# Layer 2 of a four-layer stack: the first expert tile's two weight gathers move from ahead of the scatters to behind them

## The chip, the cores and the metric

The kernel runs on one core of a Trainium2 chip. The metric is the device time of one execution, in microseconds (us), given as the median of the runs shown. All arithmetic is in fp32.

## The reference

The program is a stack of four layers over two images of 256 channels and 32 x 32 pixels, so 2 x 1024 tokens of 256 values. Layers 0 and 1 are attention over convolution features. Layer 2 is attention in windows of 64 tokens, then a mixture of eight experts. Layer 3 is additive attention, then another mixture. The change lies at the start of layer 2's mixture, which computes:

```python
logits = xt @ Wr + br
probs = jax.nn.softmax(logits, axis=-1)
top_p, top_idx = jax.lax.top_k(probs, 2)
weights = top_p / top_p.sum(axis=-1, keepdims=True)
...
xe = xn[None, :, :] * ln_g[:, None, :] + ln_b[:, None, :]
h = gelu(einsum('end,edh->enh', xe, W1) + b1[:, None, :])
y = einsum('enh,ehd->end', h, W2) + b2[:, None, :]
out = (weights[:, :, None] * y[of the two chosen experts]).sum(axis=1)
```

## The kernel before

**Routing by slots.** Each token goes to two of eight experts. `route` (L1240) computes, on the chip, a slot number for each of a token's two choices (`rt_slot0`, `rt_slot1`), so that the slots of one expert are contiguous and padded to tiles of 128, and for every slot tile the rows of the weight table that its expert owns (`rt_rows`). A group is one image: 1024 tokens, 8 token tiles, 23 slot tiles. `dispatch` (L1179) gates, routes and then writes the tokens out: for each token tile and each of the two choices one indirect DMA, issued on GpSimd (POOL), scatters 128 rows of 1 KB into `slots_in` in HBM (L1211). That is 16 scatters for a group. They are declared independent of each other.

**Experts.** `experts` (L1384) loops over the 23 slot tiles m. SyncE (SP) loads a tile of `slots_in` into `xr` (L1419), which needs the scatters of the group; TensorE transposes it (L1427), VectorE scales it into `xe` (L1431). `up` runs two halves of 16 matmuls against the up weights (L1452), VectorE adds the bias into `hb` (L1463), ScalarE applies GELU (L1441), `down` runs 16 matmuls against the down weights (L1472), and the result goes to `slots_out`.

**Weights.** A tile's expert is known only at run time, so its weights are gathered by an indirect DMA on POOL, in `fetch` (L1365, the DMA is recorded at L1370): `l2_up` with 128 rows of 2056 values, `l2_down` with 128 rows of 2048, so about 1.05 MB each. There are three pairs of buffers (`ew00`, `ew01`, `ew10` and so on); tile m uses pair m modulo 3. Where the rows say that the buffer already holds the same expert, the row numbers are out of bounds and nothing is moved. At its first step `experts` asks for the inputs of tiles 0, 1 and 2, and for up 0, down 0, up 1, down 1, up 2; what is already in `self.fetched[key]` is left out. In the loop, tile m asks for down m+2 and up m+3.

**What orders the work.** Up to the first expert tiles of layer 2, the order on POOL, SP and VectorE isn't the program's: the tile framework places instructions by their program priority and by when they become ready. In the window attention (`window_attention`, which runs `dispatch(2, 0)` as the generator `route`, a few steps in each of its last rounds) the order on TensorE and ScalarE is the program's. The rest of the stack is merged from generators by a plan with due times (`run`, L1752): `E20` is `experts(2, 0)`, due at 0; `D21` is `dispatch(2, 1)`, the other image's group, due at 5. From `E21` on, TensorE, ScalarE and VectorE keep the merged order.

**What else is on POOL there.** `divide(i)` of the window attention (L895) normalises the attention weights of token tile i in two POOL instructions (`probs`, L901), one for each half of the partitions. Those of the last tile, i = 15, come earlier in the program than the gathers and scatters. TensorE's transposes of that tile (L920), its value and output matmuls (L929, L943), VectorE's addition into `t` (L946) and then the gate of group (2, 1) (L1143, L1172) hang on them.

Of the kernel before, what the change touches and what calls it, by code (L numbers as in the profile page):

```python
# [1009 lines left out]
class Late:  # L1010
# [168 lines left out]
    def dispatch(self, *key, done=0):  # L1179

        l, b = key
        tokens = GROUPS[key]
        n = len(tokens)
        nc = self.nc
        again = self.early.tile([P, n], F32, name="again", bufs=1) if l == 2 else None
        for half in range(done, n // 4):
            yield from self.gate(l, b, half)
            if l == 2:

                mv, rs = self.last_norm  # L1190
                to = again[:, 4 * half : 4 * half + 4]
                nc.vector.tensor_tensor(to, mv[:, :, 1], rs, ALU.mult)
                nc.vector.tensor_tensor(to, to, rs, ALU.mult)
        u = self.u[key]
        if l == 2:

            rs = self.inverse_root(again, 1e-5)
            yield 3.0
            for i in range(n):
                nc.scalar.activation(u[:, i, :], u[:, i, :], AF.Identity, scale=rs[:, i : i + 1])  # L1200
            yield 5.0
        yield from self.route(key, n)
        p, shares, slots, rows = self.routes[key]
        if key == (2, 0):
            self.fetch(key, 0)
            self.fetch(key, 0, 1)

        before = []
        for i in range(n):
            for slot in slots:  # L1210
                ins = nc.gpsimd.indirect_dma_start(  # L1211
                    out=self.stack.slots_in[b % 2],
                    out_offset=bass.IndirectOffsetOnAxis(ap=slot[:, i : i + 1], axis=0),
                    in_=u[:, i, :], in_offset=None,
                ).ins
                for other in before:
                    self.tc.declare_no_dep(ins, other, reason="a slot takes one token")
                before.append(ins)
            yield None if l == 2 else 0.5
# [664 lines left out]
```

## Time and profile before

| what | us |
|---|---|
| median of three runs | 2880.11 |
| their range | 2879.3 to 2883.23 |
| the profiled execution, its own time | 2838.24 |
| its span, first to last instruction | 2836.5 |
| TensorE busy in the span | 2619.5 |
| VectorE, ScalarE, POOL busy | 1925.6, 1830.9, 1237.0 |

The profile is of one execution. Its times count from the span's first instruction, so the stretch of interest, the seam between the window attention and the experts of layer 2, lies at 1758 to 1810 us. A row of the timeline gives start, length, engine, line, operation and tiles, then in brackets how long the engine had been idle and what ended that. "POOL DMA_INDIRECT" is the instruction that issues an indirect DMA, not its transfer. "Chain" is the chain of waits that ended last, followed back from the end. PEld is TensorE's weight load, SPq an issue on SyncE's queue.

### The profile page before, as it was taken

The page shows a single profiled execution, that of the slowest core. Times are in us where ns is not written, and L with a number is a line of the kernel's source. Part 1 is how long each engine was busy: PE and PEld are TensorE (multiplying, and loading weights), DVE is VectorE, ACT ScalarE, POOL GpSimd, SP SyncE. Part 2 cuts the span into 40 slices and gives each one's busy share as a digit, 9 for nine tenths or more (in the row PEclk, how much of TensorE's full clock was granted, in tenths as well). Part 3 has the DMA queues.
Part 4 walks back from the last instruction along what each step waited for, and adds up shares of the span by engine and source line. Part 5 has one row for each costly group of instructions (what it writes and reads, how often), then busy time and mean ns, then how long its engine had stood idle before and what let it go on. Part 6 is the DMA issues. An engine that isn't in the chain of part 4 may idle for free. (4 is left out here: it accounts for less than half of the span.)

```text
span 2836.5 us, 77376 instructions
## 1 busy us (share of the span) xinstructions
PE 2619.5 (92%) x32010; PEld 1643.1 (58%) x32010; DVE 1925.6 (68%) x3579; ACT 1830.9 (65%) x2723; POOL 1237.0 (44%) x1303
## 2 busy tenths in 40 slices
PE   7899999999999999699999786899999999999997
PEld 3455555555555555455555454899666633455686
DVE  5999999999999999378778667443522343124242
ACT  2777877787787878255555343211599899989732
POOL 4877777777787777001111242343311021202152
PEclk9999999999999999899999897899999999999998
DMA  3000000000000000101110000443222010422354
GB/s 136 3 3 3 3 3 3 3 3 3 3 3 3 3 3 3 49 21 25 25 25 17 19 9 24 170 149 98 84 81 80 23 34 14 152 68 88 102 188 123
DMA packets 180705, 131.26 MB, mean 46 GB/s; under 512 B 131248, under 2 KB 162496, under 8 KB 173184
## 3 DMA queue, kind: packets, MB, share of 16 engines
q0 software_dynamic: 29232, 81.71, 8.7%
q1 hardware_dynamic: 148096, 44.25, 7.0%
q8 instruction: 251, 4.11, 0.6%
q14 instruction: 102, 0.84, 0.1%
q10 hardware_dynamic: 3024, 0.35, 0.1%
HBM read 181.11 MB, written 29.49 MB: 74 GB/s over the span
## 5 line engine op out<-in xcount | busy, mean ns | idle before, releaser
L188 ACT ACTIVATE sc<-sc,sa_shift 128x1024 f32<-128x1024 f32 x512 | 584.4, 1144 | 155.9 <-DMA sa_shift<-sa_min 153.8
L201 DVE STREAM_TRANSPOSE wt<-sc 128x1024 f32<-128x1024 f32 x512 | 601.8, 1208 | 0.2 <-ACT sc L188 0.2
L1670 ACT ACTIVATE th<-front,qb 128x1024 f32<-128x1024 f32 x512 | 539.9, 1134 | 51.4 <-PE ps_e L1679 45.3
L211 PEld LDWEIGHTS ps_o<-wt,v 128*64 128x64 f32 x8192 | 444.2, 137 | 188.0 <-issue 106.2
L143 PE MATMUL ps_s<-kT,qT 64*32 64x512 f32 x8192 | 528.0, 595 | 17.4 <-ACT sc L153 16.8
L211 PE MATMUL ps_o<-wt,v 128*64 128x128 f32 x8192 | 504.8, 276 | 26.0 <-DVE oT L372 25.4
L166 POOL TENSOR_TENSOR fold<-sc 128x512 f32<-128x512 f32 x256 | 328.8, 1285 | 196.5 <-ACT sc L153 182.7
L168 POOL TENSOR_TENSOR fold<-sc,fold 128x512 f32<-128x512 f32 x256 | 328.3, 1282 | 21.4
L153 ACT COPY sc<-ps_s 128x1024 f32<-128x1024 f32 x256 | 255.9, 1000 | 108.3 <-PE ps_s L143 55.5
L1452 PEld LDWEIGHTS ps_h<-xe,ew 128*128 128x128 f32 x2320 | 277.4, 194 | 56.6 <-issue 32.5
L150 DVE TENSOR_SCALAR_CACHE_REDUCE sc<-ps_s 128x1024 f32<-128x1024 f32 x256 | 304.6, 1190 | 7.2 <-PE ps_s L143 6.6
L1679 PE MATMUL ps_e<-th,pick 128*32 128x512 f32 x2048 | 297.6, 607 | 5.8 <-DVE sc_a L1686 4.4
L1452 PE MATMUL ps_h<-xe,ew 128*128 128x128 f32 x2320 | 293.2, 280 | 8.5 <-DVE xe L1435 7.9
L1472 PE MATMUL ps_y<-ew,h 128*128 128x256 f32 x1160 | 271.2, 383 | 3.5 <-DVE y L1476 2.2
L143 PEld LDWEIGHTS ps_s<-kT,qT 64*32 64x32 f32 x8192 | 136.2, 106 | 228.2 <-issue 161.9
L1472 PEld LDWEIGHTS ps_y<-ew,h 128*128 128x128 f32 x1160 | 212.7, 190 | 61.5 <-issue 19.6
L630 ACT ACTIVATE sc<-sc,l_least 128x1024 f32<-128x1024 f32 x128 | 146.7, 1147 | 125.8 <-DVE sc L617 125.5
L1463 DVE TENSOR_TENSOR hb<-ps_h,ew 128x512 f32<-128x512 f32 x115 | 79.4, 690 | 199.1 <-PE ps_h L1452 183.3
L1476 DVE COPY y<-ps_y 128x256 f32<-128x256 f32 x99 | 41.9, 423 | 228.1 <-PE ps_y L1472 224.0
L1441 ACT ACTIVATE h<-hb 128x512 f32<-128x512 f32 x115 | 71.5, 623 | 183.5 <-DVE hb L1463 183.4
L636 DVE STREAM_TRANSPOSE wt<-sc 128x1024 f32<-128x1024 f32 x128 | 153.3, 1224 | 46.0 <-ACT sc L630 25.4
L617 DVE TENSOR_SCALAR_CACHE_REDUCE sc<-ps_s 128x1024 f32<-128x1024 f32 x128 | 150.6, 1212 | 40.2 <-PE ps_s L609 40.0
(292 smaller groups left out, 3131.6 us busy)
## 6 DMA issues: line engine op xcount, KB each, us to landing
xr<-slots_in SPq DMA_DIRECT2D x99, 128.0 KB, 2.5
slots_out<-y SPq DMA_DIRECT2D x99, 128.0 KB, 1.7
sa_got<-sa_least SPq DMA_DIRECT2D x512, 0.5 KB, 1.8
sa_shift<-sa_min SPq DMA_DIRECT2D x512, 0.2 KB, 1.7
slots_in<-zero POOLq DMA_DIRECT2D x46, 128.0 KB, 2.6
kh<-kh SPq DMA_DIRECT2D x32, 128.0 KB, 2.3
qh<-qh SPq DMA_DIRECT2D x32, 128.0 KB, 2.3
sa_sums<-sa_total SPq DMA_DIRECT2D x244, 1.0 KB, 1.8
```

The source lines that it names most:

```text
L143: nc.tensor.matmul(ps[r][S * c : S * (c + 1), a, :].rearrange("p (b i) -> p b i", i=S), lhsT=qT[half, p, S * i : S * (i + 1)], rhs=keys[ha ...
L150: nc.vector.tensor_scalar(scores[m][0], flat[0], 1.0, None, ALU.mult, ALU.min, accum_out=least[m // 2][:, 0, h : h + 1])
L153: nc.scalar.copy(scores[m][1], flat[1])
L166: nc.gpsimd.tensor_tensor(y, a, b, ALU.subtract)
L168: nc.gpsimd.tensor_tensor(y, a, y, ALU.subtract)
L188: nc.scalar.activation(scores[m][r], scores[m][r], AF.Exp, bias=shift[m // 2][:, r : r + 1], scale=-1.0, accum_out=total[i][:, 2 * p + r, ...
L201: nc.vector.transpose(weights[i, h][:, 2 * p + r, :], x)
L211: nc.tensor.matmul(sums[i][64 * k : 64 * (k + 1)], lhsT=v[:, at % NT, 64 * (at // NT) : 64 * (at // NT + 1)], rhs=weights[i, h][:, :, S * ...
L1452: nc.tensor.matmul(ps[:, j, :], lhsT=a[:, c, at : at + P], rhs=x[:, c, :], start=(c == 0), stop=(c == CC - 1),)
L1472: nc.tensor.matmul(ps, lhsT=h[:, j, :], rhs=w2[:, j, :], start=(j == 0), stop=(j == HB - 1))
L1670: nc.scalar.activation(h, keys, AF.Tanh, bias=self.qb[b][:, s // G, g : g + 1])
L1679: nc.tensor.matmul(pe[i][c * U : (c + 1) * U, a, :], lhsT=self.pick[:, k, :], rhs=h[:, a, :], start=(k == 0), stop=(k == G - 1),)
```

## The change

After `route` has set the rows, the kernel before asks at once for both gathers of expert tile 0, ahead of the group's scatters. The changed kernel doesn't. Nothing else is edited: `experts` finds the two not fetched and issues them at its own first step, in the loop that already asks for tiles 1 and 2, after all 16 scatters.

```diff
         yield from self.route(key, n)
         p, shares, slots, rows = self.routes[key]
-        if key == (2, 0):
-            self.fetch(key, 0)
-            self.fetch(key, 0, 1)
 
         before = []
         for i in range(n):
```

The loop that now issues them, unchanged:

```python
        if l == 2:
            for m in range(lanes):
                fetch(m)
                if m < 2:
                    fetch(m, 1)
```

## Prediction

> **What bounds the kernel now.** I read four views in this order. First the chain of waits, to see which stage ends last around the change. The chain by line gives TensorE's expert matmuls (L1452, L1472) the largest shares, and the windows table shows why: once layer 2's experts run, TensorE has no idle time (columns: stretch, its length, then busy us and count of PE, PEld, DVE, ACT, POOL).
>
> ```profile
> 1795.00:1830.00 35.00, 34.39 (x233) 32.79 (x233) 15.94 (x50) 11.03 (x20) 7.97 (x8) 0.93 0.32 116
> 1830.00:1865.00 35.00, 35.00 (x248) 33.14 (x247) 14.67 (x45) 5.90 (x10) 8.97 (x9) 1.00 0.64 219
> 1865.00:1900.00 35.00, 35.00 (x247) 32.98 (x246) 17.57 (x62) 6.07 (x10) 21.13 (x21) 1.00 0.33 100
> ```
>
> So a microsecond by which the first expert tile starts earlier or later moves all 23 tiles with it, and what follows. Second, the pieces of the chain in order of time between 1740 and 1800 us, for what that start hangs on:
>
> ```profile
> 1766.46 3.45 issue
> ...
> 1786.79 2.41 DMA slots_in<-u,rt_slot
> ...
> 1789.48 4.75 DMA xr<-slots_in
> ...
> 1794.37 0.68 PE ps_x L1427 x2
> ...
> 1795.64 4.21 PE ps_h L1452 x18
> ```
>
> It hangs on the sixteenth scatter (issued 1786.79, landed 1789.2), then the load of `xr` (issued 1789.48), its transpose, the first up matmul at 1795.64. Not on weights. Third, POOL's timeline, for what delays the sixteenth scatter:
>
> ```profile
> 1763.03 0.97 POOL L1211 DMA_INDIRECT slots_in<-u,rt_slot  x1 [0.30 <-DVE rt_one L1355]
> 1764.30 1.06 POOL L1370 DMA_INDIRECT ew<-in_l_up,rt_rows  x1 [0.30 <-issue]
> 1765.43 1.03 POOL L901 TENSOR_TENSOR probs<-l,wa_rec 64x512 f32<-64x512 f32 x1
> 1770.05 1.04 POOL L901 TENSOR_TENSOR probs<-l,wa_rec 64x512 f32<-64x512 f32 x1 [3.59 <-issue]
> 1771.37 1.03 POOL L1370 DMA_INDIRECT ew<-in_l_down,rt_rows  x1 [0.28 <-POOL probs L901]
> 1772.70 1.02 POOL L1211 DMA_INDIRECT slots_in<-u,rt_slot  x1 [0.30 <-issue]
> ...
> 1786.79 0.97 POOL L1211 DMA_INDIRECT slots_in<-u,rt_slot  x1 [0.30 <-issue]
> 1788.06 1.05 POOL L1370 DMA_INDIRECT ew<-in_l_up,rt_rows  x1 [0.30 <-issue]
> ```
>
> The reader is to see both gathers of tile 0 standing in front of 12 scatters, and POOL idle for 3.59 us between the two halves of `probs`. The view says "issue", but the trace's semaphore records for POOL's sequencer hold a wait of L901 that ends at 1769.87, and the up gather's semaphore is complete at 1769.84: the second half of `probs` waits for every indirect DMA issued before it on POOL, and the gather is the last of them. Fourth, TensorE just before the start:
>
> ```profile
> 1788.82 3.75 PE L1172 MATMUL ps_router<-sb_wr,uT 128*128 128x8 f32 x16 [0.57 <-DVE uT L1144]
> 1794.37 0.66 PE L1427 MATMUL ps_x<-ident,xr 128*128 128x128 f32 x2 [1.80 <-DMA xr<-slots_in]
> ```
>
> TensorE works on the other group's gate until 1792.57 and then waits 1.80 us for `xr`. That gate is a second limit on the start.
>
> **What the Trainium skill says.** "DMA: Bandwidth & Descriptors", section "Anatomy of one DMA", prices such a DMA at 2.0 us plus its bytes over 436 GB/s: for 1.05 MB an estimate of 4.4 us. The trace has 5.5 us from the start of the 1.06 us issue instruction, so it agrees. The same page, "Queues, rings and completion order", says that an engine drains a whole packet of one queue before it turns to another. The trace fits that: `xr`, issued 1.42 us after a gather, landed at 1794.23, 0.35 us behind the gather's 1793.88, 4.75 us where the median `xr` takes 2.5. "TensorE: Matmul & The Clock Gate", section "What's actually happening", has a clock that starts at half rate and is released by a busy window of about 3.4 us in a free-running grid. The trace agrees: the clock is 0.50 from 1782.9 to 1799.95, so the first 4.3 us of expert matmuls take 421 ns each, not 275.
>
> **The change, part by part.** (a) Removed ahead of the scatters: the up gather's place on POOL, 1764.30 to the next instruction's normal start, 1.27 us (the pitch of scatters, 0.97 + 0.30); the down gather's, 1772.70 - 1771.37 = 1.33 us. (b) Removed wait: with the gather gone, a scatter takes its place at 1764.30, the first half of `probs` stays at 1765.43, and the second half waits for that scatter: 1764.30 + 2.4 (median landing) = 1766.7, plus 0.2 from semaphore to start as before, 1766.9 for 1770.05. That is 3.15 us. If `probs` comes straight after the fourth scatter the sum is the same within 0.1. (c) Sixteenth scatter: `probs` ends 1767.95, the sixth scatter starts at 1768.25, ten more pitches of 1.275 bring the sixteenth to 1781.0, for 1786.79: **5.8 us earlier**. It lands at 1783.4 and `xr` is issued at 1783.7 (call this X; before, X was 1789.48). SP's other waits there are on work of 1778.6 and before, which moves with `probs`.
>
> (d) Moved behind: six gathers now follow the scatters where four did, at 1.3 us of POOL each (1788.06, 1789.42, 1790.74 before). POOL has nothing else queued until the next gather, at 1802.74 before, so their issue is covered. Tile 0's up gather is issued at 1782.3, X - 1.4, just where tile 1's was. That row landed at X + 4.4, so tile 0's weights should land at X + 4.4, and `xr` behind them at X + 4.75. The first up matmul comes at X + 6.16, so the cover is 1.8 us. Below: nothing can be gained from a weight that wasn't waited for. Above: if the gather took the 8.5 us of the second in a row, the matmul would wait 1 us. I take zero.
>
> (e) Tile 1's up weights become third in the row. Before, the four landed at X + 4.4, 8.4, 11.0 and 13.8. Tile 1's first up matmul came after 14 of the 30 in the row at 1800.01, at 1801.65, X + 12.2. Third in the row is X + 11.0: 1.2 us of cover, and a wait of up to 1 us if the clock is full sooner. Down 0 (X + 8.4, needed X + 15.9), up 2 (about X + 16.5, needed X + 19.3) and the later ones have more.
>
> (f) What is late next: the gate. It hangs on the second half of `probs` (TensorE's L920 starts at 1771.15, 0.06 us after it), so it moves by 3.15 us, not 5.8: it ends at 1789.4, while `xr` could be transposed at 1794.37 - 5.8 = 1788.6. The start then moves by 1.80 + 3.15 = 4.95 us. If the transpose goes first, it moves by 5.8, but the 3.75 us of gate matmuls at half clock fall behind it. So 5.0 to 5.8; I take **5.3 us**. The clock is worth up to 1.7 us either way (half of one 3.4 us window), zero in the mean. From there TensorE is busy without gaps, so the end moves by the same.
>
> The profiled execution would go from 2838.24 to 2832.9. The median shown is 41.9 us above that execution; nothing in the change scales with that, so I subtract the same: 2880.1 - 5.3 = **2874.8 us**.
>
> **The rivals.** One: more gain. With the gap ahead of the start closed, the gate's matmuls and the experts' run without pause, the clock is full one window sooner, and the transpose goes first: 5.8 + 1.7 = 7.5, 2872.6 us. For it: TensorE's 1.80 us gap disappears. Against: the grid of the clock's windows isn't the program's. Two: the gathers become the wait. If the six share the DMA engines worse than the four did (at 1793 to 1796 us these were already 1.01 busy), tiles 0 and 1 wait for weights by 1 to 2 us each and about 2 us of gain stay: 2878. Three: the change doesn't do what it says, because POOL's order is by readiness (before, four scatters went ahead of a gather that stands first in the program): 2880. Four, slower: the framework, which chooses VectorE's order in advance, holds tile 0 to be late for its weights and puts the other group's routing in front of its `xe`. For it: that routing is interleaved there already. Its price: the first group's took 15.0 us from the exponential at 1743.76 to the last slot number at 1758.73. Begun at the gate's new end, 1789.4, plus 0.5 for maximum and subtraction, it puts `xe` at 1804.9 for 1795.17: 9.7 us slower, 2889.8. It decides once more than 5.7 us of routing stand in front. Against: before, most of that routing ran inside the experts (its counts matmul is at 1859).
>
> **How the numbers follow.** The forecast has 0.56, more gain 0.17, gathers as the wait 0.13, no effect 0.03, slower 0.11. A difference of 0.2%, 5.8 us, is about what a measurement of this kernel can tell from no change. The forecast's own range is 2872.5 to 2877 (the clock, and POOL's and SP's order downstream, which is placed anew), so about a third of it, 0.20, lies below 2874.3: faster 0.37, within 0.52, slower 0.11. The range goes from 2871 (rival one with a favourable order downstream) to 2880.5 (rivals two and three); outside it are rival four and about 0.07 of tails.
>
> **What would show it.** Right: on POOL 16 scatters and then six gathers in a row; 1.3 us or less of idle time between the halves of `probs`; sixteenth scatter near 1781.0, first up matmul near 1790, ended by `xe` and not by a gather; no idle TensorE after it. Wrong: a first up matmul that waits for a DMA of `ew`, gathers between the scatters, or routing instructions (L1260 to L1314) ahead of the first `xe` on VectorE.

## The result, and the profile after

The changed kernel takes 2876.42 us (median of 19 runs, 2870.28 to 2880.03) where the kernel before took 2879.44 us beside it. The ratio is 0.9984 with a 95% interval of 0.9977 to 0.9990: **4.6 us faster, 2.9 to 6.6**. (Gains below are worked out from the ratio of the runs; it isn't the quotient of the two medians, which lie 3.0 us apart.) The forecast was 5.3 us, and the time it named, 2874.8 us, is 1.6 us off.

The profiled execution of after took 2871.1 us, that of before 2838.24. Only about 6 of those 33 us are there by the middle of the first group's experts, 13 over most of the second group's and 27 over the first of layer 3's. They are not the change's: the kernel before, profiled again below, took 2831.3 us on one chip and 2879.6 on another, and those two profiles part in jumps as well. At this seam they part by 10.1 us; from tile 0 to tile 20 of the group nothing is added. So the seam is read here from the first scatter of group (2, 0): its start is subtracted from every time, and written as S + n.

The windows table of after (columns as in the prediction) shows TensorE without idle time in the experts again:

```profile
1795.00:1830.00 35.00, 34.79 (x233) 33.18 (x232) 16.97 (x56) 9.12 (x16) 6.97 (x7) 0.89 0.28 102
1830.00:1865.00 35.00, 35.00 (x242) 32.98 (x241) 15.69 (x43) 9.53 (x15) 8.96 (x9) 1.00 0.61 215
```

POOL's timeline of after:

```profile
1768.76 0.97 POOL L1208 DMA_INDIRECT slots_in<-u,rt_slot  x1 [0.30 <-DMA slots_in<-u,rt_slot]
1769.79 1.03 POOL L901 TENSOR_TENSOR probs<-l,wa_rec 64x512 f32<-64x512 f32 x1
1771.41 1.04 POOL L901 TENSOR_TENSOR probs<-l,wa_rec 64x512 f32<-64x512 f32 x1 [0.59 <-DMA slots_in<-u,rt_slot]
...
1780.41 0.97 POOL L1208 DMA_INDIRECT slots_in<-u,rt_slot  x1 [0.30 <-issue]
1781.68 1.06 POOL L1367 DMA_INDIRECT ew<-in_l_up,rt_rows  x1 [0.31 <-issue]
...
1788.27 1.00 POOL L1367 DMA_INDIRECT ew<-in_l_down,rt_rows  x1 [0.30 <-issue]
```

The sixteenth scatter starts at 1780.41, S + 22.3 (S is 1758.13), where it was S + 28.0, and six gathers follow in a row. The 3.6 us wait between the halves of `probs` has shrunk to 0.59. But nine scatters now stand ahead of `probs`, not four, so its second half comes at S + 13.3 instead of S + 11.3: later, not earlier.

The chain of waits of after, in order of time (start, length, what):

```profile
1778.35 4.77 issue
1783.12 3.06 PE ps_wo L943 x4
...
1786.33 8.14 DMA xr<-slots_in
1794.47 0.14 issue
1794.61 0.66 PE ps_x L1424 x2
1795.27 2.79 PE ps_router L1172 x14
1798.05 4.05 PE ps_h L1449 x18
```

It no longer runs through the sixteenth scatter. Further back it runs through the ninth, for which the second half of `probs` waited (1771.41). Then it runs through the last window tile's output projection (L943), the load of `xr`, its transpose, and then through **14 router matmuls of the other group's gate**, which now stand between the transpose and the first up matmul. TensorE's order has changed. Before, both halves of that gate (each 8 transposes, L1143, and 16 router matmuls, L1172) stood ahead of the first tile's transpose. Now the second half lies between the expert tiles; its last piece on TensorE's timeline of after:

```profile
1834.46 1.85 PE L1172 MATMUL ps_router<-sb_wr,uT 128*128 128x8 f32 x16
```

### The profile page after: what moved, and what is told of

Read it like the earlier page. It is cut to its first block, busy times and chain, and to the rows that moved or that the text cites. A ratio compares the mean times of both kernels' runs of the same rounds, so it can differ in the third digit from the quotient of the medians.

```text
span 2869.4 us, 77379 instructions
## 1 busy us (share of the span) xinstructions
PE 2628.3 (92%) x32010; PEld 1645.6 (57%) x32010; DVE 1925.7 (67%) x3579; ACT 1835.4 (64%) x2725; POOL 1237.8 (43%) x1303
## 5 line engine op out<-in xcount | busy, mean ns | idle before, releaser
L1449 PEld LDWEIGHTS ps_h<-xe,ew 128*128 128x128 f32 x2320 | 278.6, 195 | 63.2 <-issue 36.5
L1473 DVE COPY y<-ps_y 128x256 f32<-128x256 f32 x99 | 41.9, 424 | 230.3 <-PE ps_y L1469 213.4
L617 DVE TENSOR_SCALAR_CACHE_REDUCE sc<-ps_s 128x1024 f32<-128x1024 f32 x128 | 150.6, 1212 | 40.0 <-PE ps_s L609 39.8
```

The source lines that it names most:

```text
L1449: nc.tensor.matmul(ps[:, j, :], lhsT=a[:, c, at : at + P], rhs=x[:, c, :], start=(c == 0), stop=(c == CC - 1),)
```

## Experiments

Theory one, of the **scatters**: the sixteenth scatter sets the start of the experts, as the prediction had it. Theory two, of **probs**: with nine scatters ahead of it, the last window tile's chain has become the limit. Theory three, of the **placement**: the seam gained nothing, and the gain comes from the order of later work. Two more, of the **cover** and of the **order**, came out of the first runs.

The copy `y` that ends a tile (L1473, before L1476) is a marker for what the seam is worth: from tile 5 to the end of the group it keeps a constant distance to the kernel before. All runs stand in one table, with times as S + n. "Up" is the first up matmul's start, "gained" how much earlier `y` of tile 5 comes than in the kernel before on a chip of the same kind, and "ratio" the time over that of the kernel before, run beside it.

| kernel | 16th scatter | transpose | up | y of tile 5 | gained | ratio (95%) |
|---|---|---|---|---|---|---|
| **chip with runs near 2835** | | | | | | |
| before | 28.2 | 35.7 | 36.9 | 86.5 | | 0.9999 (0.9989 to 1.0008) |
| changed | 22.3 | 29.6 | 32.9 | 86.0 | 0.5 | 0.9997 (0.9988 to 1.0005) |
| changed, early probs | 22.2 | 29.7 | 31.0 | 83.2 | 3.3 | 0.9983 (0.9972 to 0.9994) |
| before, early probs | 24.9 | 32.5 | 33.7 | 83.2 | 3.3 | 0.9988 (0.9980 to 0.9995) |
| **chips with runs near 2880** | | | | | | |
| before | 28.0 | 45.6 | 46.9 | 96.6 | | |
| changed (the result) | 22.3 | 36.5 | 39.8 | 92.8 | 3.8 | 0.9984 (0.9977 to 0.9990) |
| up gather alone | 26.7 | 35.4 | 40.4 | 92.1 | 4.5 | 0.9980 (0.9970 to 0.9989) |
| down gather alone | 26.7 | 36.1 | 40.4 | 92.3 | 4.3 | 0.9977 (0.9966 to 0.9988) |
| changed, early probs, gate first | 22.2 | 45.6 | 46.8 | 96.6 | 0.0 | 1.0008 (1.0000 to 1.0016) |
| changed, gate first | 22.3 | 47.0 | 48.3 | 97.5 | -1.0 | 0.9999 (0.9992 to 1.0006) |
| before, TensorE's order | 28.0 | 35.4 | 43.4 | 95.7 | 0.9 | 0.9994 (0.9985 to 1.0002) |
| before, order of both engines | 28.0 | 35.7 | 37.3 | 89.4 | 7.2 | 0.9969 (0.9961 to 0.9977) |
| changed, early probs | 22.1 | 37.4 | 41.7 | 93.4 | 3.1 | 0.9983 (0.9973 to 0.9992) |

### Both kernels again, and probs early

No edit for the first two.

> The kernel before once more, unchanged, for a profile that can be laid beside that of the changed kernel (the profiled execution of before shown first was 33 us shorter than that of the changed kernel, far more than the 4.6 us between their runs). All theories expect the ratio to lie at 1.000 with an interval of about 0.2%, which says what a ratio of this many rounds can tell. In its profile: sixteenth scatter of the first group about 28 us after the first (28.0 in the first profile), second half of the last window tile's probs waiting some 3.6 us for the up gather, the first up matmul of the first expert tile about 37 us after the first scatter (36.9 in the first profile). If the later dispatches are long again only where the whole execution is, the 33 us are the execution's and not the change's.

> The changed kernel once more, for a second profile and more rounds. Theory of the scatters (the sixteenth scatter sets the start of the first expert tile): ratio 0.998, first up matmul 5 us nearer to the first scatter than in the kernel before. Theory of the probs (the scatters come 6 us earlier, but nine of them now stand ahead of the second half of probs, so that the turn of the first tile waits for the gate and for the window projection's psum): ratio 0.998 to 0.999, and in the profile the xr load is released by TensorE's window projection and not by the sixteenth scatter; the scatters are done 2 us or more before that. Theory of the placement (the order of the work later on moved, and the seam itself gained nothing): first up matmul at the same distance from the first scatter as before, the gain further on.

For the other two, `divide` keeps its second half's instruction, and the scatters from the fourth on and the gathers are held behind it; the last one does the same to the kernel before:

```diff
+                    late.halves = nc.gpsimd.tensor_tensor(
...
+                behind = key == (2, 0) and len(before) >= 3
+                with self.tc.issue_after(self.halves) if behind else nullcontext():
                     ins = nc.gpsimd.indirect_dma_start(
...
+        with self.tc.issue_after(self.halves) if key == (2, 0) else nullcontext():
             self.nc.gpsimd.indirect_dma_start(
```

> The changed kernel with GpSimd's order held: three scatters, then both halves of the last window tile's probs, then the other thirteen scatters and the six gathers. Nothing is left out. Theory of the probs: probs' second half ends about 7 us earlier than in the changed kernel (estimate 1764.6 against 1772.45 where the first scatter is at 1758.1), the window projection and the gate with it, the sixteenth scatter stays near 1780.2, the xr load is issued behind the scatters at about 1783 instead of 1786.3, the first up matmul comes 3 to 5 us earlier: ratio to the kernel before 0.9965 to 0.9975, 3 to 5 us faster than the changed kernel. Theory of the scatters: the sixteenth scatter is where it was, so the time is that of the changed kernel, 0.998. Theory of the placement: the ratio is anything between 0.997 and 1.001 and does not follow the seam.

> The kernel before, both gathers of the first tile still ahead of the scatters that follow, but the two gathers and the scatters from the fourth on held behind the second half of the last window tile's probs. Nothing is left out. It takes the wait for the up gather away and leaves the gathers' places on GpSimd: sixteenth scatter estimated at 1782.8 on the clock of the first profile of before, where it was 1786.8. Theory of the scatters: 4.0 us faster than before, ratio 0.9986. Theory of the probs: the same or slightly more, as the gate comes early too, 0.998 to 0.9986, about 1.5 to 2.6 us slower than the changed kernel with the same hold. Theory of the placement: no relation to the seam, 0.997 to 1.001.

Measured: on this chip the median of before was 2835.5 us. The two profiles of before near 2835 us agree to 0.2 us in the table's columns. The changed kernel's gain was 0.9 us, and the interval, from 3.4 faster to 1.4 slower, includes none. The theories of the scatters and of probs had expected 0.998 and 0.998 to 0.999. TensorE's timeline of the changed kernel here:

```profile
1789.02 0.66 PE L1424 MATMUL ps_x<-ident,xr 128*128 128x128 f32 x2 [5.83 <-DMA xr<-slots_in]
1789.47 2.99 PE L1172 MATMUL ps_router<-sb_wr,uT 128*128 128x8 f32 x14
1792.32 4.19 PE L1449 MATMUL ps_h<-xe,ew 128*128 128x128 f32 x18
...
1828.88 1.85 PE L1172 MATMUL ps_router<-sb_wr,uT 128*128 128x8 f32 x16
```

The transpose waits for `xr`, and `xr` was issued 2.7 us behind the sixteenth scatter, as the theory of the scatters has it; the transpose is 6.0 us earlier. Then 14 router matmuls stand ahead of the up matmul, which starts 3.3 us after the transpose where it was 1.3: 2.0 us lost. The gate's second half takes 3.24 more between the tiles (transposes 0.41, 0.38 and 0.60, routers 1.85). 6.0 - 2.0 - 3.2 leaves 0.8, and `y` of tile 5 shows 0.5. With early probs the first half is done long before, only the second half is paid, and 3.3 us stay; in the kernel before with early probs both halves fit ahead of the transpose, and it keeps all 3.3 us of its earlier scatter. So the theory of the scatters holds here for the transpose, not for the end. The two holds have about the ratios that this theory named (0.998 and 0.9986), but it had named 0.998 for the changed kernel too, whose sixteenth scatter is as early as with early probs and whose interval includes no gain. The theory of probs had wanted 0.9965 to 0.9975 with early probs. None of the three had the reason: **work that had run in TensorE's idle time now has to be paid.** This is the theory of the cover.

### The gate first, one gather alone, and before once more

The first kernel adds to the early probs that both halves of the gate come ahead of the first tile's transpose. `D21` becomes due 32 earlier and its routing waits 32 longer, so that the gate alone moves in the program; `self.gated` is the gate's last router matmul:

```diff
-            "D21": (self.dispatch(2, 1), (), 5, 3.45),
+            "D21": (self.dispatch(2, 1), (), -27, 3.45),
...
+        if key == (2, 1):
+            yield 32.0
         yield from self.route(key, n)
...
+            with self.tc.issue_after(self.gated) if key == (2, 0) and m == 0 else nullcontext():
                 for c in range(CC):
                     nc.tensor.transpose(ps[:, c, :], r[:, c * P : (c + 1) * P], self.ident)
```

> The changed kernel with GpSimd's order held as in the run with probs behind three scatters, and in addition the whole gate of the other group (both halves: 16 transposes and 32 router matmuls of the 48 on TensorE there) held ahead of the transpose of the first expert tile. Nothing is left out. Theory of the cover (the gate's second half ran in TensorE's idle time at the seam before; in the changed kernel and in the run with the earlier probs it falls behind the first tile's transpose, where TensorE has no idle time, and costs its own 2.4 to 3.0 us there): the transpose stays at 29.7 us after the first scatter, the gate's second half runs from about 22 to 28.5 us after it, the copy y of tiles 4 to 22 comes 5.4 to 6.0 us earlier than in the kernel before, relative to the first scatter, where the run with the earlier probs had 3.3: ratio 0.9978 to 0.9982. Theory of the scatters alone: as the run with the earlier probs, 3.3 us, 0.9983 to 0.9988. Theory of the placement: the lead at tile 4 is lost again later and the ratio is 0.999 or more.

The next two are the kernel before without one of its two early gathers:

```diff
         if key == (2, 0):
-            self.fetch(key, 0)
             self.fetch(key, 0, 1)
```

> One part alone: only the up gather of the first tile is moved behind the scatters; the down gather stays. Nothing is left out. Theory of the wait (any gather of weights ahead of the second half of probs on GpSimd costs the same wait): the down gather takes the up gather's place ahead of probs, the second half waits about 3.6 us as before, and the sixteenth scatter comes only one place earlier, 1.3 us (26.9 us after the first scatter for 28.2); ratio 0.9993 to 0.9998. If the wait goes with the up gather alone: sixteenth scatter 4.5 us earlier, ratio 0.998 to 0.999. Theory of the placement: no relation to the seam.

> The other part alone: only the down gather of the first tile is moved behind the scatters; the up gather stays where it was. Nothing is left out. All theories of the seam: the wait of probs' second half stays at 3.6 us, the sixteenth scatter comes one place, 1.3 us, earlier; the transpose of the first tile is limited by the gate, which ended 1.3 us ahead of it, so at most 1.3 us: ratio 0.9993 to 1.0. Together with the run above: the two parts alone sum to 2.6 us at the sixteenth scatter where both together gave 5.8; the 3.2 us left are the wait, which goes only when both go.

> The kernel before for a profile on this chip, beside the three above. All theories: sixteenth scatter 28.2 us and first up matmul 36.9 us after the first scatter, as in the two earlier profiles of before, if the chip's transfers are as fast as there; if its executions are slower (2880 instead of 2835), all distances at the seam that end in a transfer are longer, and those of the changed kernel's first profile can then be read against these.

These went to a chip where the kernel before takes 2879.4 us, as in the runs of the result, and every ratio expected for the gate and the single gathers missed. The wait did what was expected of it: with the up gather gone the down gather stood in its place, and the second half of `probs` waited 3.52 us. The sixteenth scatter came only 1.3 us earlier. Yet the kernels without the early up gather and without the early down gather gained 5.8 us (3.2 to 8.6) and 6.6 us (3.5 to 9.8), no less than both together. With the gate first, the sixteenth scatter came 5.8 us earlier and there was no gain. On these chips the time doesn't follow the scatters at all.

The profile of before there says why. TensorE's timeline, first on the chip near 2835, then on the one near 2880:

```profile
1783.76 1.94 PE L1143 MATMUL ps_tr<-ident,u 128*128 128x128 f32 x8 [3.33 <-DVE u L1132]
1786.27 3.75 PE L1172 MATMUL ps_router<-sb_wr,uT 128*128 128x8 f32 x16 [0.57 <-DVE uT L1144]
1791.32 0.66 PE L1427 MATMUL ps_x<-ident,xr 128*128 128x128 f32 x2 [1.30 <-DMA xr<-slots_in]
```

```profile
1797.24 1.94 PE L1143 MATMUL ps_tr<-ident,u 128*128 128x128 f32 x8 [8.14 <-DVE u L1132]
1799.75 3.75 PE L1172 MATMUL ps_router<-sb_wr,uT 128*128 128x8 f32 x16 [0.57 <-DVE uT L1144]
1803.35 0.67 PE L1427 MATMUL ps_x<-ident,xr 128*128 128x128 f32 x2
```

On the first, the gate's second half ends 1.3 us before `xr` comes. On the second it starts 11.4 us later after the first scatter (S is 1755.67 and 1757.77), and the transpose follows it without a wait: the first tile stands behind the gate. What delays the gate shows on VectorE, in the addition that takes the first half's router matmuls:

```profile
1780.47 0.19 DVE L1176 TENSOR_TENSOR rt_lg<-ps_router,sb_br 128x32 f32<-128x32 f32 x1 [1.72 <-PE ps_router L1172]
```

```profile
1794.40 0.19 DVE L1176 TENSOR_TENSOR rt_lg<-ps_router,sb_br 128x32 f32<-128x32 f32 x1 [8.15 <-remote]
```

By the trace those matmuls ended at 1780.43 and at 1789.10, so they were taken over after 0.04 us on one chip and after 5.3 us on the other. VectorE itself wasn't late: in the semaphore records of the second trace TensorE's count arrives at 1794.38, and the addition starts 0.02 us later. In all, the addition is 11.8 us later after the first scatter than on the first chip; some 6.5 us had been lost before it, on TensorE's and VectorE's work from the output projection on. The chain that prepares the second half (inverse root, scaling of `u`) stands behind this instruction on VectorE. The theory of the **order** follows: near 2880 us, time is set by whether the first tile stands behind the second half of that gate. Moving a gather, either one, made the framework place it otherwise.

### The order alone

Two kernels test that, one from each side. In the first no gather is moved; the gate's second half is held behind the first tile's transpose:

```diff
+                last = nc.tensor.transpose(ps[:, c, :], r[:, c * P : (c + 1) * P], self.ident)
+            if key == (2, 0) and m == 0:
+                self.first_turn = last.ins
...
+            with self.tc.issue_after(self.first_turn) if key == (2, 1) and 4 in tiles else nullcontext():
                 for k, i in enumerate(tiles):
                     nc.tensor.transpose(ps[:, k, :], self.u[key][:, i, c * P : (c + 1) * P], self.ident)
```

> The kernel before with its gathers where they were, and one thing changed: on TensorE the second half of the other group's gate (8 transposes, 16 router matmuls counted as the profile counts passes) is held behind the transpose of the first expert tile, where the changed kernel has it, instead of ahead. Nothing is left out. Theory of the order (what moved the time on the chip with runs near 2880 us is that the first tile no longer stands behind that half of the gate on TensorE; on the chip with runs near 2835 us the gate fitted into idle time and is only paid for elsewhere): near 2880 us, the first up matmul comes 6 to 8.5 us earlier relative to the first scatter, of which about 3 are paid back by the gate between the tiles, ratio 0.998 to 0.999, with no gather moved; near 2835 us, the first up matmul is where it was and the tiles from 5 on come 2.5 to 3 us later, ratio 1.0008 to 1.0012. Theory of the scatters: the sixteenth scatter is where it was, so no gain on either chip, 1.000 to 1.001.

The second is the changed kernel with the hold of "gate first" and nothing else.

> The changed kernel with one thing undone: on TensorE the whole gate of the other group is held ahead of the transpose of the first expert tile, as in the kernel before. The gathers stay behind the scatters. Nothing is left out. Theory of the order: the gain goes with it. Near 2880 us, first up matmul and y of tile 5 within 1 us of the kernel before relative to the first scatter, ratio 0.9995 to 1.0005, 4 us slower than the changed kernel; near 2835 us, transpose of the first tile 35.4 us after the first scatter instead of 29.6, y of tile 5 within 0.5 us of before, ratio 0.9998 to 1.0005. Theory of the scatters: the sixteenth scatter is as early as in the changed kernel, so its gain stays, 0.998 to 0.9985 near 2880 us.

Both ran on a chip near 2880. With the gate first the changed kernel's gain is gone: 0.9999, where the theory of the scatters wanted 0.998. (The up matmul came 1.4 us later than in the kernel before, where at most 1 was expected.) The other side missed its ratio: 0.9994, with an interval that includes no gain, where 0.998 to 0.999 was expected. The transpose came 10.2 us earlier with the gathers where they were, but the up matmul only 3.4, where 6 to 8.5 were expected. VectorE and then TensorE there:

```profile
1796.29 1.38 DVE L1132 TENSOR_SCALAR u<-t,n_mv,ir_y 128x256 f32<-128x256 f32 x4
1800.30 0.73 DVE L1434 TENSOR_SCALAR xe<-ps_x,rt_affine 128x128 f32<-128x128 f32 x2
```

```profile
1800.76 3.78 PE L1455 MATMUL ps_h<-xe,ew 128*128 128x128 f32 x16 [2.89 <-DVE xe L1434]
```

The up matmul waited for `xe`, which stood on VectorE behind the chain for the gate's second half. In the changed kernel `xe` stands ahead of that chain. So the last kernel holds VectorE's order too (`behind` is true for that half of the gate alone):

```diff
+        with self.tc.issue_after(self.first_xe) if behind else nullcontext():
             self.scale(dst, src, tiles, mv)
```

> The kernel before with its gathers where they were, and the order at the start of the first expert tile as the changed kernel has it on both engines: on TensorE the second half of the other group's gate behind the first tile's transpose, and on VectorE the chain that prepares it (inverse root and the scaling of u, L1106 to L1132) behind the first xe. Nothing is left out. It follows the run in which TensorE's order alone was changed, where the first up matmul came 3.4 us earlier and then waited 2.9 us for xe behind that chain on VectorE. Theory of the order: near 2880 us, first up matmul about 37.5 to 39 us after the first scatter where it was 46.8, about 3 us of it paid back by the gate between the tiles, y of tile 5 earlier by 4 to 6 us, ratio 0.998 to 0.9986, as much as or more than the changed kernel gains, with no gather moved; near 2835 us, first up matmul where it was, y of tile 5 later by 2.5 to 3 us, ratio 1.0006 to 1.0012. Theory of the scatters: no gain on either, as the sixteenth scatter stays 28 us after the first.

> The changed kernel with probs held behind three scatters, once more, on whichever chip this is. Nothing is left out. Near 2835 us as before: y of tile 5 3.3 us earlier than in the kernel before, ratio 0.998 to 0.9988. Near 2880 us (theory of the order: the first tile stands behind the first half of the other group's gate alone, and that is earlier than in the changed kernel): first up matmul 37 to 38.5 us after the first scatter where the changed kernel had 39.8, y of tile 5 4 to 6.5 us earlier than in the kernel before, ratio 0.9977 to 0.9986, the same as the changed kernel or up to 2.5 us faster. Theory of the scatters: as the changed kernel, since the sixteenth scatter is where it was.

Near 2880 again. With no gather moved, the order alone gains **8.9 us, 6.6 to 11.2**, more than the change:

```profile
1793.51 0.66 PE L1430 MATMUL ps_x<-ident,xr 128*128 128x128 f32 x2 [3.61 <-DMA xr<-slots_in]
1795.15 3.78 PE L1460 MATMUL ps_h<-xe,ew 128*128 128x128 f32 x16 [0.98 <-DVE xe L1437]
```

The transpose is at S + 35.7, as on the chip near 2835 (S is 1757.86), and now waits for `xr`. The up matmul is 9.6 us earlier, slightly more than expected, `y` of tile 5 by 7.2, also above the 4 to 6 expected, and so is the gain itself (0.9969 for 0.998 to 0.9986). The changed kernel with early probs gained 4.9 us (2.3 to 7.8), within the expected ratio, but its up matmul, at S + 41.7, was 3.2 us later than the latest expected, and `y` of tile 5 gained 3.1 instead of 4 or more: the first half of its gate was itself late (its routers waited 8.17 us for `uT`). That version gains on both kinds of chip. The order of both engines was run near 2880 alone; near 2835 it should lose the 3.2 us of the gate, which wasn't tried, nor was it tried together with early probs.

## Why the prediction came out right

**The number is right, and the reason half; that the two met is luck.** On the kind of chip whose profile the prediction argued from, the same change gained 0.9 us and not 5.3. Near 2880 it gained 4.6, but there the start hung on something else. (a) The two places on POOL: right; each gather alone gave 1.3 us at the sixteenth scatter. (b) The removed wait: right that a gather ahead of `probs` costs it; the runs add that either gather does, so that moving one alone leaves it. Wrong that `probs` would follow the fourth or fifth scatter: it fell behind nine, and came 2.0 us later instead of 3.15 earlier. (c) Sixteenth scatter 5.8 us earlier: it was 5.8 near 2835 and 5.7 near 2880.

(d) and (e) Gathers behind the scatters at no cost: right near 2835, not quite near 2880. Near 2835 the six landed 4.1, 8.1, 10.9, 13.7, 16.2 and 19.1 us after the issue of `xr`; the prediction had 4.4 for the first and 11.0 for the third. No up matmul of the first tiles waited for weights on either chip. But near 2880 `xr` was issued only behind the output projection, at S + 28.2, when four gathers had been issued. The third of them landed 8.0 us after the issue of `xr`, and `xr` itself 0.2 us behind that gather, after 8.1 us where the prediction had 4.75. TensorE waited 1.99 us for it ahead of the transpose. So the rival of weights as the new wait is out, but the gathers did delay the first tile's input there. The rival of routing ahead of the first `xe` is out.

(f) **The step that failed.** The sign that the prediction set for itself, a first up matmul near 1790 (about S + 31), missed: it came at S + 32.9 near 2835 and at S + 39.8 near 2880. The prediction named the gate as what is late next and even said that, if the transpose goes first, the gate falls behind it. But it took the start to move by 5.0 to 5.8 and, with "from there TensorE is busy without gaps, so the end moves by the same", charged nothing for the gate afterwards. The same sentence says why that is wrong: behind the start there is no idle time, so work pushed there is paid in full. Measured: the up matmul moved by 4.0 us near 2835 and by 7.1 near 2880, and 3.5 and 3.3 of it were paid back by tile 5. The forecast of 5.3 stood near the 4.6 measured because, near 2880, a larger gain (leaving the delayed gate) was reduced by a cost that it left out.

**What it could not see.** The profile of before was of an execution of 2838.24 us, the runs near 2880. The prediction put that offset down to nothing in the change. At the seam it was not neutral: near 2880 the binding chain was another one, the gate and not the scatter. That the up matmul stood behind the gate there is shown by the order kernels, from both sides. That the offset was the chip's is an inference from four chips, on each of which all kernels kept near its time.

What stays open is why the first half of the gate is late near 2880. VectorE's addition that takes it over starts there at S + 36.2 to S + 40.0 in all nine profiles, with early probs too; near 2835 it starts at S + 24.8 in the kernel before, S + 19.3 with early probs and S + 33.1 in the changed kernel. The Trainium skill, "Perfetto Trace Analysis", section "Tensor Engine Instruction (MATMUL, LD_WEIGHTS)", says that a matmul's end in the profile is an estimate, and that its semaphore is pushed once PSUM, the memory that matmuls write to, has acknowledged the bytes. In the profile of before near 2880 the signal came 5.3 us behind that estimate, so that trace can't tell a late matmul from a late signal. Nor was the gain of the changed kernel near 2835, 0.9 us with zero in its interval, settled as different from none.

## What to carry to other kernels

When a start is brought forward, list what ran in the idle time ahead of it: work that ends up behind the start, on an engine without gaps, costs its full time there. Where a scheduler places the instructions, compare each engine's order at the seam before and after a change; holding that order alone, with nothing else changed, shows whether the change or the order did it. And compare a profile's own time with the runs first: 1.5% between them can mean that another chain binds.

## What the runs showed of the hardware

- The same program took 2835.5 us on one chip and 2879.4, 2880.6 and 2881.1 on three others (medians of the kernel before).
- At the same instruction, the time from the end of a matmul in the profile to the addition that takes its result was 0.04 us on one chip and 5.3 us on another; there TensorE's semaphore came 0.02 us before the addition.
- The kernel before was 10.1 us later on a chip near 2880 than on one near 2835 at tile 0 after this seam, and still 10.1 us at tile 20: this part of the difference arose at the seam, not inside the row of expert tiles.
- A compute instruction on POOL waited for the gather issued just ahead of it whichever gather that was: 3.5 to 3.7 us behind an up or a down gather, 0.4 to 0.6 behind scatters alone.
- Six gathers of 1.05 MB issued 1.3 us apart landed 2.5 to 4.0 us apart. The first load of `xr`, 128 KB, took 8.1 us where four gathers had been issued ahead of it (the changed kernel near 2880) and 4.75 us where two had (the profile in the prediction).
